# The experts' small side tasks in two parts: what TensorE multiplies for them stands behind the next expert's first up products

## The chip, the core and the metric

The kernel runs on one core of a Trainium2 chip. A core has a matrix engine (TensorE, PE in the profile; its weight loads are shown as PEld), VectorE (DVE), ScalarE (ACT), GpSimd (POOL), and SyncE (SP), which here only issues DMAs. Each engine works through its own list of instructions in order and waits at semaphores for the others. Matrix products land in PSUM, a small memory of banks; everything else lives in SBUF or in device memory (HBM, "dram" in names). The metric is the device time of one execution in microseconds (us). A profiled execution also gives every instruction's start and length, and the TensorE clock that was granted, as a share of full speed.

## The reference

Two layers, on x of 4 x 512 x 512 (2048 tokens of 512):

```python
x = x + _L0_xattn_ref(ctx_1024, _layernorm(x), ...)       # a state-space scan over time
x = x + _L0_ffn_ref(_layernorm(x), gate, gate_up, down, similarity)   # experts
x = x + _L1_xattn_ref(_layernorm(x), ctx_1024, Wq, Wk, Wv, Wo, gq, gk) # attention
x = x + _L1_ffn_ref(_layernorm(x), w1, w2)                 # ternary weights, 8-bit activations
```

The part around the change is the second line. Each token picks 8 of 64 experts by a softmax over gate logits; some of the picks are mapped to a similar expert; then each expert computes on its tokens

```python
gu = lax.ragged_dot(xs, swapaxes(gate_up_proj, 1, 2), group_sizes)   # 512 -> 2 x 192
gate, up = jnp.split(gu, 2, axis=-1)
y = lax.ragged_dot(jax.nn.silu(gate) * up, swapaxes(down_proj, 1, 2), group_sizes)
out = jnp.zeros_like(x).at[tok].add(y * w[:, None])
```

Three things that later stages need are computed beside the experts: the weight of each pick and the row where its y lies; the mean of |w1| and of |w2| and the rounded ternary weights of the last line; and the inverse norms of the attention's keys.

## The kernel before, in words

The order of instructions on each engine is the order in which the Python code calls them: the phase stands under a manual schedule (moe_phase), and no planner moves anything in it. Pools decide only when a buffer may be written again.

The experts' loop (Experts.run_in, lines 1373 to 1391) has 66 turns, one more for each stage of a pipeline over 64 experts. The experts are sorted by size and have fixed room, from 352 rows down to 232, in tiles of 128 rows. Turn i does, in this order:

- issues on POOL's queue the gathers of expert i+2's rows (xg) and weights (wg, wd), four buffers each (line 1223);
- for m = 0, 1, 2: the up products of expert i-1 (gate_up, line 1282, eight instructions into a PSUM tile pg of which there are three), and then the transposes of one tile of expert i's rows (turn_x, line 1266) into a PSUM tile pt, copied to xT by ScalarE, or by VectorE for tile 1 (line 1269). Silu is on ScalarE (1286, 1288), the product h on VectorE (1289, 1291);
- in the first turns, a key task (pk, line 1182);
- the down products of expert i-2 (po, lines 1306 to 1316), whose copies yo are stored to y_dram by SP (1328);
- side tasks from a list (line 1388), until the number done has reached (i-1)/54 of them;
- keys.squares, the sums of squares of the key task's result (kpss, line 1202).

So an expert's h is used one turn after it was made, and so is xT. The PSUM tag "pt" has two buffers in turn; the transposes of the rows, the key tasks and all side tasks share them.

The side tasks are called one after the other, and each ran as a whole. Most have no TensorE work. Those that have some prepare an operand on another engine first:

- many (1470): one small product. Not touched by the change.
- row (1475), twice: VectorE makes a diagonal s_diag, TensorE multiplies ones with it (prow, 1479), VectorE copies the row.
- remap (1497), four times: TensorE transposes four blocks of wt (pwT, 1501), ScalarE copies them to s_wT (1503), TensorE multiplies by the map of experts (pw, 1506), ScalarE copies back to wt (1507).
- mean (1757), twice: VectorE sums the parts of a weight matrix (wone, 1759), TensorE sums over partitions (pm, 1761), VectorE makes the scale of it (1762, 1763). The tasks add and round_ around it read the weights w1 and w2 in eight pieces each.
- key_norms (1551): step 0 loads the sums of squares to krk (SP, 1556); step 1 takes 1/sqrt of them (rsqrt, line 90: a root on ScalarE, for which it loads a table, and five VectorE operations, lines 96 to 100); steps 2 and 3 transpose 128 and 64 columns of it (kpt, 1563), copy them to krows on ScalarE (1565) and store them to r_dram on SP (1570). The pool that holds krows and s_wT has one buffer of each.

After the loop the program reads one number (the blocks of rows that found no room) and branches on it; here the branch is not taken. Attention then starts by gathering y rows (line 1823).

Of the kernel before, what the change touches and what calls it, by code (L numbers as in the profile page):

```python
# [17 lines left out]
F32 = mybir.dt.float32  # L18
# [6 lines left out]
ALU = mybir.AluOpType  # L25
# [4 lines left out]
P = 128  # L30
B, S, DM = 4, 512, 512
NT = B * S // P
NC = DM // P
CTX = 256
EPS = 1e-5
DS, DC, DR = 16, 4, 16
NG = 4
E, TOPK, SEL, FI = 64, 8, 4, 192
# [22 lines left out]
DH = 2048  # L61
# [28 lines left out]
def rsqrt(nc, pool, out, v, tag):  # L90

    shape = list(out.shape)
    r = pool.tile(shape, F32, name=f"rs_r_{tag}", tag=f"rs_r_{tag}")
    t = pool.tile(shape, F32, name=f"rs_t_{tag}", tag=f"rs_t_{tag}")
    nc.scalar.activation(t, v, AF.Sqrt)
    nc.vector.reciprocal(r, t)
    nc.vector.tensor_tensor(t, r, r, ALU.mult)
    nc.vector.tensor_tensor(t, t, v, ALU.mult)
    nc.vector.tensor_scalar(t, t, -0.5, 1.5, ALU.mult, ALU.add)
    nc.vector.tensor_tensor(out, r, t, ALU.mult)  # L100
# [1230 lines left out]
class Experts:  # L1331
# [24 lines left out]
    def run_in(self, ctx, tern, more, late, keys, kv):  # L1356
        cm, ex, st = self.cm, self.ex, self.st
        tc = cm.tc
        ex.sp = ctx.enter_context(tc.tile_pool(name="e_s", bufs=2))
        ex.yp = ctx.enter_context(tc.tile_pool(name="e_y", bufs=3))  # L1360
        ex.ps = ctx.enter_context(tc.tile_pool(name="e_ps", bufs=2, space=PSUM))
        ex.pg = ctx.enter_context(tc.tile_pool(name="e_pg", bufs=3, space=PSUM))
        ex.po = ctx.enter_context(tc.tile_pool(name="e_po", bufs=3, space=PSUM))
        tp = ctx.enter_context(tc.tile_pool(name="e_t", bufs=2))
        kp = ctx.enter_context(tc.tile_pool(name="e_k", bufs=1))
        key_list, ctx_k = key_tasks(keys, self.w, kp, late, ex.ps)
        slots, norms = slot_tasks(cm, self.dr, kv, self.r, more, ex.ps)
        tasks = slots + tern.tasks(tp, ex.ps) + norms
        many = len(tasks)
        done = 0  # L1370
        QUOTA = 54
        self.load_rows(0)
        self.load_rows(1)
        for i in range(E + 2):
            self.load_rows(i + 2)
            self.load_weights(i + 2)
            keys.take()
            for m in range(3):
                if 1 <= i <= E:
                    ex.gate_up(st[i - 1], m)  # L1380
                if i < E:
                    ex.turn_x(st[i], m)
            if i >= 2 and key_list:
                key_list.pop(0)()
            if i >= 2:
                ends = list(range(ROWS[i - 2], ROWS[i - 1], P)) + [ROWS[i - 1]]
                ex.down(st[i - 2], [self.y_dram[r0:r1, :] for r0, r1 in zip(ends, ends[1:])])
                while tasks and done < (i - 1) * many / QUOTA:
                    tasks.pop(0)()
                    done += 1  # L1390
            keys.squares()
        assert not tasks and not key_list
        return ctx_k


# [33 lines left out]
def slot_tasks(cm, dr, kv, r, pool, ps):  # L1429


    nc = cm.nc
    vec, gp, act, pe = nc.vector, nc.gpsimd, nc.scalar, nc.tensor
    c = {}
    codes, chosen = r["codes"], r["chosen"]
    wt = r["weights"] = pool.tile([P, NT, E], F32, name="wt")
# [38 lines left out]
    def row(name):  # L1475
        d = pool.tile([E, E], F32, name="s_diag")
        vec.tensor_scalar(d, cm.ident[0:E, 0:E], c[name], None, ALU.mult)
        pp = ps.tile([P, E], F32, name="prow", tag="pt")
        pe.matmul(pp, cm.ones[0:E, :], d, start=True, stop=True)
        c[name] = pool.tile([P, E], F32, name=f"s_{name}_row")  # L1480
        vec.tensor_copy(c[name], pp)

    def load():
        nc.sync.dma_start(wt, dr["z"][:, :, 0, 0:E].rearrange("t p e -> p t e"))
# [12 lines left out]
    def remap(q):  # L1497
        at = slice(q * NC, (q + 1) * NC)
        pt = ps.tile([E, NC, P], F32, name="pwT", tag="pt")
        for j in range(NC):  # L1500
            pe.transpose(pt[:, j, :], wt[:, q * NC + j, :], cm.ident)
        wT = pool.tile([E, NC, P], F32, name="s_wT")
        act.copy(wT, pt)
        pw = ps.tile([P, NC, E], F32, name="pw", tag="pt")
        for j in range(NC):
            pe.matmul(pw[:, j, :], wT[:, j, :], r["map"], start=True, stop=True)
        act.copy(wt[:, at, :], pw)

    def inside(n):

# [38 lines left out]
    n = sum(c1 - c0 for c0, c1 in cols)  # L1549

    def key_norms(step):
        if step == 0:
            c["rk"] = pool.tile([P, n], F32, name="krk")
            at = 0
            for c0, c1 in cols:
                nc.sync.dma_start(c["rk"][:, at:at + c1 - c0], kv["ms"][:, c0:c1])
                at += c1 - c0
        elif step == 1:
            rsqrt(nc, pool, c["rk"], c["rk"], "k")
        else:  # L1560
            a0, a1 = (step - 2) * P, min((step - 1) * P, n)
            pt = ps.tile([P, P], F32, name="kpt", tag="pt")
            pe.transpose(pt[0:a1 - a0, :], c["rk"][:, a0:a1], cm.ident)
            rows = pool.tile([P, P], F32, name="krows")
            act.copy(rows[0:a1 - a0, :], pt[0:a1 - a0, :])
            at = 0
            for c0, c1 in cols:
                lo, hi = max(at, a0), min(at + c1 - c0, a1)
                if lo < hi:
                    nc.sync.dma_start(kv["r"][c0 + lo - at:c0 + hi - at, :],  # L1570
                                      rows[lo - a0:hi - a0, :])
                at += c1 - c0

    calls = [(load,), (rooms,), (many,), (row, "limit"), (row, "first"), (weigh, 0), (weigh, 1)]
    calls += [(inside, n) for n in range(4)] + [(tops, q) for q in range(NT // NC)]
    calls += [(remap, q) for q in range(NT // NC)]
    calls += [(weight, k, i) for k in range(TOPK) for i in range(3)] + [(finish,)]
    norms = [(key_norms, i) for i in range(2 + -(-n // P))]
    return [[lambda f=f, a=a: f(*a) for f, *a in part] for part in (calls, norms)]

# [136 lines left out]
class Ternary:  # L1717
# [8 lines left out]
    def tasks(self, pool, ps):  # L1726


        cm, nc = self.cm, self.cm.nc

        L = NC * DH // (2 * NC)

        def load(n, c):
            t = pool.tile([P, L], F32, name="wf")
            if n == 0:
                nc.sync.dma_start(t, self.w["w1T"][c // 2 * P:(c // 2 + 1) * P,
                                                   c % 2 * L:(c % 2 + 1) * L])
            else:
                k = L // DM
                src = self.w["w2T"].rearrange("(k p) o -> p k o", p=P)  # L1740
                nc.sync.dma_start(t.rearrange("p (k o) -> p k o", k=k),
                                  src[:, c * k:(c + 1) * k, :])
            return t

        loads = [(n, c) for n in range(2) for _ in range(2) for c in range(2 * NC)]
        ready = []

        def fetch():
            if loads:
                ready.append(load(*loads.pop(0)))  # L1750

        def add(n, c):
            nc.vector.tensor_reduce(self.part[n][:, c:c + 1], ready.pop(0), AX.X, ALU.add,
                                    apply_absolute_value=True)
            fetch()

        def mean(n):
            one = pool.tile([P, 1], F32, name="wone")
            nc.vector.tensor_reduce(one, self.part[n], AX.X, ALU.add)
            pm = ps.tile([P, 1], F32, name="pm", tag="pt")  # L1760
            nc.tensor.matmul(pm, cm.ones, one, start=True, stop=True)
            nc.vector.tensor_scalar(self.mean[n], pm, 1.0 / (DM * DH), EPS, ALU.mult, ALU.max)
            nc.vector.reciprocal(self.ws[n], self.mean[n])

        def round_(n, c):
            t = ready.pop(0)

            nc.vector.tensor_scalar(t, t, self.ws[n], 1.0, ALU.mult, ALU.min)
            nc.vector.tensor_scalar(t, t, -1.0, MAGIC, ALU.max, ALU.add)
            nc.scalar.activation(self.out[n][:, c * L:(c + 1) * L], t, AF.Copy, bias=-MAGIC)  # L1770
            fetch()

        nc.vector.tensor_copy(self.identb, cm.ident)
        calls = [(fetch,), (fetch,)]
        for n in range(2):
            calls += [(add, n, c) for c in range(2 * NC)] + [(mean, n)]
            calls += [(round_, n, c) for c in range(2 * NC)]
        return [lambda f=f, a=a: f(*a) for f, *a in calls]
# [593 lines left out]
```

## Time and profile before

| | |
|---|---|
| three runs | 2628.28, 2637.88, 2644.03 us; median 2637.88 us |
| the profiled execution | 2642.93 us, of which the instructions span 2641.2 us |
| granted TensorE clock, mean over the span | 0.97 |
| scan and routing | 0 to about 640 us |
| experts | about 640 to 1355 us |
| attention and the last layer | about 1360 to 2641 us |
| DMA | 395.77 MB, mean 150 GB/s |

Stretches of the experts' stage (columns: length, busy time of PE, DVE, ACT and POOL, granted clock, share of the time that the DMA engines were busy):

| us | length | PE | DVE | ACT | POOL | clock | DMA |
|---|---|---|---|---|---|---|---|
| 640 to 1262 | 622 | 606.93 | 230.12 | 175.91 | 253.67 | 0.99 | 0.75 |
| 1262 to 1345 | 83 | 77.70 | 21.17 | 23.77 | 27.89 | 0.96 | 0.67 |

An engine's busy time says how much it did, not whether it was waited for. The list of waits puts the idle time of an engine in front of an instruction down to what ended it: "PE pw L1506 <- ACT s_wT L1503" reads: TensorE, at the product pw of line 1506, waited for ScalarE's instruction that writes s_wT in line 1503. A list in order of time gives start and length of runs of equal instructions; their lengths overlap a little with the next run's start, since products are pipelined.

### The profile page before, as it was taken

The numbers are of one execution on the slowest core, as the hardware profiler recorded it, in microseconds if no ns is written. First come the engines' busy times: TensorE is split into PE (matmuls) and PEld (weight loads), VectorE is DVE, ScalarE is ACT, GpSimd is POOL, SyncE is SP. The second block draws the span as 40 slices with busy tenths as digits, with TensorE's granted clock in tenths as the row PEclk, the third lists the DMA queues.
The fourth block names the chain that finished last, engine by engine and source line by source line (L and its number), as shares of the span: only waits on it lengthen the run. The fifth ranks groups of instructions, "written<-read, shape, count | busy, mean of one in ns | idle before, by whom it ended". The sixth has DMA issues, their size and how long they took to land. (4 is left out here: it accounts for less than half of the span.)

```text
span 2641.2 us, 29732 instructions
## 1 busy us (share of the span) xinstructions
PE 2474.5 (94%) x10020; PEld 1404.2 (53%) x10071; DVE 1485.0 (56%) x2562; ACT 1237.6 (47%) x2359; POOL 1180.7 (45%) x1108
## 2 busy tenths in 40 slices
PE   6989899987999999999987999999999999999997
PEld 3555556645555666566653454445555555555543
DVE  6999999854322433344225545456665666555446
ACT  6777777654232222233222444454554555554543
POOL 7999999803333444444325232134322343221112
PEclk8999999988999999999998999999999999999999
DMA  5263444326565677899764534233332443221200
GB/s 206 90 215 113 174 167 161 111 106 201 173 225 171 223 221 259 272 333 328 235 212 139 156 122 122 80 99 98 126 92 84 132 125 95 84 82 59 58 26 21
DMA packets 196143, 395.77 MB, mean 150 GB/s; under 512 B 30339, under 2 KB 71363, under 8 KB 191888
## 3 DMA queue, kind: packets, MB, share of 16 engines
q1 hardware_dynamic: 152926, 238.85, 27.0%
q0 software_dynamic: 41008, 154.76, 18.5%
q8 instruction: 83, 1.36, 0.2%
q10 hardware_dynamic: 2050, 0.18, 0.1%
q14 instruction: 76, 0.62, 0.1%
HBM read 313.88 MB, written 79.82 MB: 149 GB/s over the span
## 5 line engine op out<-in xcount | busy, mean ns | idle before, releaser
L1936 DVE TENSOR_REDUCE mx<-psc 128x1 f32<-128x512 f32 x256 | 176.7, 690 | 460.7 <-PE psc L1933 460.7
L1282 PE MATMUL pg<-xT,wg 128*128 128x284 f32 (+12 forms) x1536 | 399.7, 405 | 2.2 <-ACT xT L1269 1.1
L1282 PEld LDWEIGHTS pg<-xT,wg 128*128 128x128 f32 x1536 | 283.0, 194 | 86.1 <-issue 36.9
L1939 ACT ACTIVATE e<-psc,mx 128x512 f32<-128x512 f32 x256 | 176.0, 687 | 309.2 <-DVE mx L1936 308.9
L492 POOL TENSOR_TENSOR dBu<-bb,du 128x1024 f32<-128x1024 f32 x128 | 303.1, 2388 | 4.4 <-DVE dA L517 3.5
L1223 POOL DMA_INDIRECT xg<-xn_dram,tok x168 | 173.5, 1033 | 215.9 <-PE pt L1266 173.8
L1933 PE MATMUL psc<-kT,qT 128*128 128x512 f32 x512 | 267.5, 604 | 1.0 <-ACT qT L1927 1.0
L1960 PE MATMUL po<-eT,v 128*128 128x512 f32 x512 | 231.4, 595 | 8.5 <-ACT eT L1954 8.4
L1899 PE MATMUL pq<-Wq,xnT 128*128 128x512 f32 x512 | 235.0, 603 | 0.7 <-ACT xnT L1858 0.7
L1969 PE MATMUL px<-Wo,oT 128*128 128x512 f32 x512 | 231.9, 597 | 0.0
L1910 POOL TENSOR_SCALAR qms<-qms 128x4 f32<-128x4 f32 x64 | 24.8, 388 | 413.3 <-DVE qms L1908 412.5
L1953 PEld LDWEIGHTS pet<-ident,e 128*128 128x128 f32 x1024 | 127.9, 142 | 146.3 <-issue 119.9
L503 ACT ACTIVATE dA<-delta,negA 128x512 f32<-128x512 f32 x256 | 176.4, 694 | 52.1 <-DVE hc L518 31.1
L517 DVE TENSOR_TENSOR_SCAN dA<-dA,dBu 128x1024 f32<-128x1024 f32 x80 | 186.5, 2331 | 16.9 <-ACT dA L503 6.6
L1327 DVE COPY yo<-po 128x512 f32<-128x512 f32 x68 | 47.0, 691 | 219.2 <-PE po L1316 219.2
L1960 PEld LDWEIGHTS po<-eT,v 128*128 128x128 f32 x512 | 96.5, 190 | 134.4 <-issue 116.0
L1823 POOL DMA_INDIRECT yg<-y_dram,pos x124 | 125.0, 1008 | 87.3 <-issue 63.4
L1953 PE MATMUL pet<-ident,e 128*128 128x128 f32 x1024 | 155.3, 275 | 7.7 <-DVE e L1945 7.7
L523 PEld LDWEIGHTS yT<-ident,hc 128*128 128x128 f32 x1024 | 117.7, 142 | 79.2 <-issue 40.9
L1223 POOL DMA_INDIRECT wd<-down,widx x64 | 62.7, 980 | 200.5 <-PE po L1316 178.4
L523 PE MATMUL yT<-ident,hc 128*128 128x128 f32 x1024 | 131.6, 276 | 21.5 <-DVE yg L557 9.6
L1954 ACT COPY eT<-pet 128x512 f32<-128x512 f32 x256 | 148.0, 578 | 6.3 <-PE pet L1953 6.1
(355 smaller groups left out, 4375.5 us busy)
## 6 DMA issues: line engine op xcount, KB each, us to landing
y_dram<-yo SPq DMA_DIRECT2D x110, 256.0 KB
bb<-bc_dram SPq DMA_DIRECT2D x16, 1024.0 KB
cb<-bc_dram SPq DMA_DIRECT2D x16, 1024.0 KB
v_dram<-v SPq DMA_DIRECT2D x64, 256.0 KB
k_dram<-k_kT SPq DMA_DIRECT2D x64, 256.0 KB
Wq<-Wq SPq DMA_DIRECT2D x16, 1024.0 KB
kT<-k_dram SPq DMA_DIRECT2D x64, 256.0 KB
rk<-r_dram SPq DMA_DIRECT2D x64, 256.0 KB
```

The lines of the kernel that those rows point to most:

```text
L492: nc.gpsimd.tensor_tensor(dBus[q], st[b]["bb"][i // 2][:, j:j + 2, :], st[b]["du"][c].unsqueeze(1).to_broadcast([P, 2, S]), ALU.mult)
L503: nc.scalar.activation(dAs[q][:, j, :], st[b]["delta"][c], AF.Exp, scale=negA[:, c, n:n + 1])
L517: nc.vector.tensor_tensor_scan(*flat, 0.0, ALU.mult, ALU.add)
L523: nc.tensor.matmul(yT[:, lc, :], t[:, lc * P:(lc + 1) * P], cm.ident, is_transpose=True, start=first and lc == 0, stop=last, skip_group_ch ...
L1223: nc.gpsimd.indirect_dma_start(out=t[0:n, :], out_offset=None, in_=table, in_offset=bass.IndirectOffsetOnAxis(ap=index, axis=0))
L1282: nc.tensor.matmul(pg[:, 0:n], s["wg"][:, c, m * P:(m + 1) * P], s["xT"][:, c, 0:n], start=c == 0, stop=c == NC - 1)
L1899: nc.tensor.matmul(pq.rearrange("p h d -> p (h d)"), xnTs[b * NC + i][:, c, :], s["Wq"][:, c, :], start=c == 0, stop=c == NC - 1)
L1933: nc.tensor.matmul(pscore, st[b, g]["qT"][:, h, i * P:(i + 1) * P], ks[n], start=True, stop=True)
L1936: nc.vector.tensor_reduce(mx, pscore, AX.X, ALU.max, negate=True)
L1953: nc.tensor.transpose(pt[:, kc, :], e[:, kc * P:(kc + 1) * P], cm.ident)
L1960: nc.tensor.matmul(po, v[:, kc, :], eT[:, kc, :], start=kc == 0, stop=kc == KB - 1)
L1969: nc.tensor.matmul(px, oTs[j * HG + h][:, i * P:(i + 1) * P], st[b, g]["Wo"][:, h, :], start=h == 0, stop=h == HG - 1)
```

## The change

A task may now return a function, left, with what remains to be done. The loop keeps it (held), takes no further task in this turn, and calls it in the next turn between the first up products (m = 0) and the first transposes of rows. Row, remap and mean return what begins with their TensorE product; for remap, the transposes and the first copy stay in the task. Step 1 of key_norms returns an empty function, which does nothing but end the turn's tasks. The list of tasks and the pace of 54 are the same; a turn that was cut short is made up for in later ones.

In the lists of the engines this moves: prow (twice), pw (four times) and pm (twice) on TensorE behind the next expert's first up products (the eight instructions of m = 0), with the copies that follow them on VectorE and ScalarE; the four remaps, two of which stood behind one expert, to four experts in a row; the first two products of the task weight on VectorE one expert later; the first kpt with its copy and its store one expert later, so that both kpt stand behind the same expert. POOL's list has the same order as before; on SP only the first store to r_dram changes its place, past two stores to y_dram.

```diff
@@ run_in
+        held = []
@@
             for m in range(3):
                 if 1 <= i <= E:
                     ex.gate_up(st[i - 1], m)
+                if m == 0 and held:
+                    held.pop()()
                 if i < E:
                     ex.turn_x(st[i], m)
@@
-                while tasks and done < (i - 1) * many / QUOTA:
-                    tasks.pop(0)()
+                while tasks and not held and done < (i - 1) * many / QUOTA:
+                    left = tasks.pop(0)()
                     done += 1
+                    if left is not None:
+                        held.append(left)
@@ row
-        pp = ps.tile([P, E], F32, name="prow", tag="pt")
-        pe.matmul(pp, cm.ones[0:E, :], d, start=True, stop=True)
-        c[name] = pool.tile([P, E], F32, name=f"s_{name}_row")
-        vec.tensor_copy(c[name], pp)
+
+        def left():
+            pp = ps.tile([P, E], F32, name="prow", tag="pt")
+            pe.matmul(pp, cm.ones[0:E, :], d, start=True, stop=True)
+            c[name] = pool.tile([P, E], F32, name=f"s_{name}_row")
+            vec.tensor_copy(c[name], pp)
+        return left
@@ remap
-        pw = ps.tile([P, NC, E], F32, name="pw", tag="pt")
-        for j in range(NC):
-            pe.matmul(pw[:, j, :], wT[:, j, :], r["map"], start=True, stop=True)
-        act.copy(wt[:, at, :], pw)
+
+        def left():
+            pw = ps.tile([P, NC, E], F32, name="pw", tag="pt")
+            for j in range(NC):
+                pe.matmul(pw[:, j, :], wT[:, j, :], r["map"], start=True, stop=True)
+            act.copy(wt[:, at, :], pw)
+        return left
@@ key_norms
         elif step == 1:
             rsqrt(nc, pool, c["rk"], c["rk"], "k")
+            return lambda: None
@@ mean
-            pm = ps.tile([P, 1], F32, name="pm", tag="pt")
-            nc.tensor.matmul(pm, cm.ones, one, start=True, stop=True)
-            nc.vector.tensor_scalar(self.mean[n], pm, 1.0 / (DM * DH), EPS, ALU.mult, ALU.max)
-            nc.vector.reciprocal(self.ws[n], self.mean[n])
+
+            def left():
+                pm = ps.tile([P, 1], F32, name="pm", tag="pt")
+                nc.tensor.matmul(pm, cm.ones, one, start=True, stop=True)
+                nc.vector.tensor_scalar(self.mean[n], pm, 1.0 / (DM * DH), EPS, ALU.mult, ALU.max)
+                nc.vector.reciprocal(self.ws[n], self.mean[n])
+            return left
```

More of the change, by code (lines that the diff above doesn't have):

```diff
@@ L1387, in run_in @@
                 ex.down(st[i - 2], [self.y_dram[r0:r1, :] for r0, r1 in zip(ends, ends[1:])])
-                while tasks and done < (i - 1) * many / QUOTA:
-                    tasks.pop(0)()
+                while tasks and not held and done < (i - 1) * many / QUOTA:
+                    left = tasks.pop(0)()
                     done += 1
+                    if left is not None:
+                        held.append(left)
             keys.squares()
-        assert not tasks and not key_list
+        assert not tasks and not key_list and not held
         return ctx_k
```

## The prediction

> **What bounds the kernel now.** I read the page's head and its table of slices first, then TensorE's list of waits in the experts' stage, then the stage's instructions in order of time. The page:
>
> ```profile
> span 2641.2 us, 29732 instructions
> PE 2474.5 (94%) x10020; PEld 1404.2 (53%) x10071; DVE 1485.0 (56%) x2562; ACT 1237.6 (47%) x2359; POOL 1180.7 (45%) x1108
> ```
>
> TensorE is busy 94% of the span, the next engine 56%. The chain of waits cannot be followed through the experts: after them the program branches on a loaded number, and the chain's pieces begin at 1362.08 us. So the stage (about 640 to 1355 us) is judged by who waits for whom in it. From the list of waits between 580 and 1300 us, all engines (microseconds in total, times, longest):
>
> ```profile
> POOL xg L1223 <- PE pt L1266: 173.8, 76, 10.8
> POOL wd L1223 <- PE po L1316: 163.4, 54, 6.5
> ```
>
> The gathers of rows and weights wait for TensorE to give buffers back. In the other direction, TensorE alone:
>
> ```profile
> PE kpt L1563 <- DVE krk L100: 5.3, 1, 5.3
> PE pm L1761 <- DVE wone L1759: 5.2, 2, 3.0
> PE pt L1266 <- DMA xg<-xn_dram,tok: 4.6, 3, 3.0
> PE pw L1506 <- ACT s_wT L1503: 3.9, 4, 1.4
> PE pk L1182 <- DVE xT L1269: 2.9, 1, 2.9
> PE prow L1479 <- DVE s_diag L1477: 2.0, 2, 1.0
> ```
>
> The 4.6 us for a transfer lies before 700 us; later TensorE waits for no DMA. Between 640 and 1262 us it is busy 606.93 of 622 us. It therefore sets the pace, and four of these six rows (kpt, pm, pw, prow) are the small tasks that the change splits. The same places in order of time (start, length, engine and line, work, in brackets the idle time before it):
>
> ```profile
> 674.77 0.40 PE L1479 MATMUL prow<-s_diag,ones 64*128 64x64 f32 x2 [0.97 <-DVE s_diag L1477]
> 675.10 1.05 PE L1202 MATMUL kpss<-ones,k_sq 128*128 128x1 f32 x8
> 676.01 4.14 PE L1282 MATMUL pg<-xT,wg 128*128 128x328 f32 x8
> 680.43 2.37 PE L1282 MATMUL pg<-xT,wg 128*128 128x328 f32 x8
> ...
> 795.07 1.33 PE L1506 MATMUL pw<-map,s_wT 64*128 64x64 f32 x8 [1.37 <-ACT s_wT L1503]
> 796.34 3.69 PE L1282 MATMUL pg<-xT,wg 128*128 128x300 f32 x8
> 800.30 2.19 PE L1282 MATMUL pg<-xT,wg 128*128 128x300 f32 x8
> ...
> 813.29 1.97 PE L1506 MATMUL pw<-map,s_wT 64*128 64x64 f32 x8 [0.72 <-ACT s_wT L1503]
> 815.18 4.26 PE L1282 MATMUL pg<-xT,wg 128*128 128x292 f32 x8
> ...
> 831.39 2.23 PE L1282 MATMUL pg<-xT,wg 128*128 128x292 f32 x8
> ```
>
> Beside the bracketed gap there is a second loss: the same eight products take 3.69 us behind one gap and 2.19 us four microseconds later. The granted clock was 0.83 in 800 to 820 us and 1.00 in 840 to 860. The largest place:
>
> ```profile
> 1268.33 0.45 PE L1563 MATMUL kpt<-ident,krk 128*128 128x128 f32 x1 [5.30 <-DVE krk L100]
> 1268.57 3.41 PE L1282 MATMUL pg<-xT,wg 128*128 128x240 f32 x8
> ...
> 1279.79 1.79 PE L1282 MATMUL pg<-xT,wg 128*128 128x240 f32 x8
> ```
>
> **The change part by part.** The sum is made against the profiled execution's 2642.93 us (2641.2 us span, 1.7 us around it), which is 5.05 us above the median 2637.88 us of the three runs.
>
> *Split tasks.* The preparation on VectorE or ScalarE stays where it was; TensorE passes to the next expert's first up products (pg, about 1.8 to 2.3 us) and does the task's products after them. A gap shorter than that goes whole, a longer one shrinks by one pg. No product is added.
> - row, twice: gaps of 0.97 and 1.03 us, both shorter than pg (2.2 us): 2.00 us.
> - remap, four times: 1.37 + 0.94 + 0.72 + 0.90 = 3.93 us, pg is 2.1 us: all gone. Two stood behind one expert; now each has its own.
> - mean, twice: gaps of 3.00 and 2.19 us. VectorE finishes wone (1090.39 and 1199.60 us) some 2.9 and 2.0 us after the last down product, behind a 1.22 us sum of its own, whatever TensorE does. One pg covers 1.86 and 1.76 us (start to start); 1.14 and 0.43 us stay in front of pm, with the turns queued behind it. Gain 3.62 us.
> - key_norms' rsqrt, which only sends its transpose one expert on: ScalarE loads a table (1263.72, 1.28 us) and takes the root, VectorE needs five operations until 1268.23. TensorE idled 5.30 us and now has an expert's whole work (some 8.7 us) meanwhile. Gain 5.30 us.
>
> Idle time: 14.85 us. The part within mean is the least sure: between 1160 and 1260 us the DMA share is 0.86 to 1.01, and VectorE waits 7.2 us there for ternary weights, so of the second mean's 1.76 us anything from all to nothing may come back as a later wait.
>
> *The clock.* Slow products behind the gaps, by printed lengths against the same shape at full rate: 676.01 us: 4.14 - 2.37 = 1.77. Remap: pw 1.33 - 1.10 and 1.97 - 1.10, pg 3.69 - 2.19 and 4.26 - 2.23, one turn 0.83 - 0.60, together 4.86. At 1268.57 us: 3.41 - 1.79, then a turn 1.06 - 0.60 and a pg 2.30 - 1.79, together 2.59. Sum 9.22 us. Not every gap cost it: the gaps at 693, 830, 1090 and 1199 us, one of them 3.00 us, were followed by full rate. Hence bounds 0 and 9.22. I take 9.22, since no gap is left at these three places, and the low-work stretch that stays (kpss, 1.05 us) stands in front of full-rate pg at 653.67 us too.
> [...]
>
> *Moved and new waits.* Both transposes of key_norms now stand behind one expert. Their copies go to one krows buffer (bufs=1), so ScalarE's second copy waits for the DMA that stores the first, and that DMA is issued on SP behind two y_dram stores, one place later than before. Queued behind the copy on ScalarE: the next silu and xT. TensorE's second turn needs the PSUM buffer that the copy frees. Before, the store to r_dram was issued at 1281.38, 1.73 us after the last down product (1279.65), and that turn began at 3.82 us; with another transpose, 4.07. The landing isn't in the trace: from below, the y_dram store of the chain at 1362.19 us, 2.76 us; from above, the gathers' median of 5.8 us (wd). With some 0.35 us for the copy the turn could start at 4.85 to 7.9 us: a stall of 0.8 to 3.8 us. I take 2.0, nearer to the store, which is the same kind of DMA. A clock loss behind it is 0 (gaps of 2.19 and 3.00 us) to 1.26 us (pk at 665.51 us, behind a gap of 2.92 us, took 3.25 us; 1.99 at 685.76); I take 0.
> - VectorE's first two slot products (1.23 us each) move one expert on and stand there with the reduction (1.22): 3.7 us between the yo copies and h, where two took 2.45 us. VectorE was idle 1.11 us ahead of h, which is used an expert later, so 0; without that cover 1.2 us once.
> - ScalarE's copy of pw now stands behind the silu: 0.37 us ahead of xT, used an expert later: 0.
> - POOL's order is unchanged; its gathers follow TensorE. On SP only that r_dram store moves, past two y_dram stores.
>
> Sum: -14.85 - 9.22 + 2.0 = -22.1 us, so 2620.8 us profiled and 2637.88 - 22.1 = **2615.8 us** as a median.
>
> **Rivals.**
> 1. *The slow products were not the gaps' doing* (small products, or a fixed rhythm of the clock): only the 5.30 us gap frees its 2.59 us. The full-rate rows after 693 and 830 us speak for it, the coincidence at three places against. -14.85 - 2.59 + 2.0 = -15.4 us: 2622.4 us. With no clock back at all and the new stall at 3.8 + 1.26 us: -9.8, 2628.1 us. [...]
> 2. *Hidden anyway*: transfers set the stage's pace and TensorE's gaps merely move. Then about 2637.9 us. For it: DMA share 1.00 at 1160 to 1200 us. Against it: POOL's 337 us of waits for TensorE, and no wait of TensorE for a DMA after 700 us.
> 3. *Slower*: attention's start. Between 1345 and 1440 us TensorE is busy 74.73 of 95 us at a granted 0.86, in short bursts between gathers; a shifted arrival could make the slow clock coincide with all of them. At clock c the busy time is 74.73 x 0.86 / c. To cancel 22 us it must be 95 + 22, so c = 0.55; at 0.50, the lowest granted of any stretch (1268 to 1271 us), it is 128.5 us, net +11 us: 2649 us. Slower than before only below 0.55 throughout, which nothing here shows.
>
> **How the numbers follow.** My forecast 0.70 (its own range 2609 to 2625: at best 14.85 + 9.22 - 0.8 = 23.3 us, at worst 22.1 less 1.76 for the second mean, 1.8 for the longer stall and 1.26 for its clock, 17.3 us; and 5 us either way, since three runs of one kernel spread 16 us). Rival 1: 0.15, half of it beyond 0.5%. Rival 2: 0.10. Rival 3: 0.05. Half a per cent, 13.2 us, is about what runs of this kernel can tell from no change; so the bounds are 2624.7 and 2651.1 us. Faster: 0.70 x 0.97 + 0.075 + 0.02 = 0.77; slower: 0.04; same: the rest, 0.19. The range runs from 2605 to 2630 us: forecast, rival 1 and the noise.
>
> **What would show it.** Right: no idle time in front of prow and pw; about 1.1 and 0.4 us left before pm; kpt twice in a row without a wait; first pg rows at 1.8 to 2.4 us everywhere; the last down product some 22 us earlier, and attention as long as before. The new wait: a turn waiting 1 to 4 us for ScalarE's krows right after the transposes. Wrong: pg rows of 3 to 4 us still behind prow or pw (rival 1), new waits of TensorE for xg, wg or h (rival 2), or a longer stretch between experts and attention (rival 3).

## The result, and the profile after

The changed kernel takes 2615.97 us (median of 8 runs, 2611.18 to 2621.17). The kernel before, run beside it, takes 2642.12 us (median of 8, 2628.28 to 2646.78). The ratio is 0.9907, 95% interval 0.9889 to 0.9924: 24.6 us faster, between 20 and 29 us. The profiled execution spans 2612.2 us.

The head of the page, after:

```profile
span 2612.2 us, 29785 instructions
PE 2469.2 (95%) x10071; PEld 1396.4 (53%) x10071; DVE 1486.6 (57%) x2562; ACT 1237.5 (47%) x2359; POOL 1179.6 (45%) x1108
```

The work is the same; the span is shorter. Three rows of TensorE's list of waits after, between 580 and 1300 us:

```profile
PE pk L1182 <- DVE xT L1269: 2.9, 1, 2.9
PE pt L1266 <- ACT krows L1577: 2.9, 1, 2.9
PE pm L1776 <- DVE wone L1772: 1.3, 2, 1.0
```

The rows of kpt (5.3 us), pw (3.9) and prow (2.0) are gone, pm's went from 5.2 to 1.3 us, and one row is new: a turn of the rows that waits for ScalarE's copy krows. (The row of 4.6 us for transfers, xg, isn't in this execution either; in before it lay ahead of 630 us, in a part that the change doesn't touch.) In order of time, TensorE after, at the first row, at two remaps and at the norms:

```profile
672.51 2.45 PE L1282 MATMUL pg<-xT,wg 128*128 128x328 f32 x8
674.89 0.43 PE L1486 MATMUL prow<-s_diag,ones 64*128 64x64 f32 x2
...
787.92 2.19 PE L1282 MATMUL pg<-xT,wg 128*128 128x300 f32 x8
790.03 1.10 PE L1516 MATMUL pw<-map,s_wT 64*128 64x64 f32 x8
...
801.07 2.13 PE L1282 MATMUL pg<-xT,wg 128*128 128x292 f32 x8
803.13 1.10 PE L1516 MATMUL pw<-map,s_wT 64*128 64x64 f32 x8
...
1252.92 0.44 PE L1575 MATMUL kpt<-ident,krk 128*128 128x128 f32 x2
1253.20 1.79 PE L1282 MATMUL pg<-xT,wg 128*128 128x240 f32 x8
...
1259.91 0.61 PE L1266 MATMUL pt<-ident,xg 112*128 112x112 f32 x4 [2.87 <-ACT krows L1577]
```

There are no brackets in front of prow and pw, and every pg runs at full rate (2.45, 2.19, 2.13 and 1.79 us, where before had 4.14, 3.69, 4.26 and 3.41). What the new wait is made of is seen on ScalarE after:

```profile
1253.55 0.27 ACT L1577 COPY krows<-kpt 128x128 f32<-128x128 f32 x1
1259.60 0.26 ACT L1577 COPY krows<-kpt 64x128 f32<-64x128 f32 x1 [5.78 <-DMA r_dram<-krows]
```

The second copy waited 5.78 us for the store of the first, which SP issued at 1254.64 us: 5.0 us from issue to the second copy's start.

To see where the 29.0 us between the two profiled spans lie, the span is cut at two points: the end of the first shown expert's down products (653.74 us before) and the end of the last one's (1358.80 us before), 62 experts apart.

| us | before | after | difference |
|---|---|---|---|
| ahead of the experts | 653.74 | 651.61 | -2.1 |
| 62 experts | 705.06 | 683.69 | -21.4 |
| behind them | 1282.40 | 1276.90 | -5.5 |

The change touches only the middle row. Whether the other two belong to it is one of the questions below.

### The profile page after: what moved, and what is told of

It reads as the page before. It is cut to its first block, busy times and chain, and to the rows that moved or that the text cites. A ratio compares the mean times of both kernels' runs of the same rounds, so it can differ in the third digit from the quotient of the medians.

```text
span 2612.2 us, 29785 instructions
## 1 busy us (share of the span) xinstructions
PE 2469.2 (95%) x10071; PEld 1396.4 (53%) x10071; DVE 1486.6 (57%) x2562; ACT 1237.5 (47%) x2359; POOL 1179.6 (45%) x1108
## 4 chain that ended last, share of the span: by engine, by line
PE 42%; DVE 3%; DMA 2%; ACT 1%; issue 1%; POOL 1%; DVEq 0%; POOLq 0%; ACTq 0%; SPq 0%
PE po L1976 9%; PE psc L1949 8%; PE px L1985 8%; PE pq L1915 7%; PE pet L1969 4%; PE pf L2085 2%; PE ph L2051 2%; DMA yg<-y_dram,pos 1%; PE pqt L1942 1%; DVE mx L1952 1%; DVE e L1961 1%; PE pk L1182 1%; PE pth L2015 0%; DMA out<-y 0%; DVE x_all L1847 0%
## 5 line engine op out<-in xcount | busy, mean ns | idle before, releaser
L1282 PE MATMUL pg<-xT,wg 128*128 128x284 f32 (+12 forms) x1536 | 392.6, 399 | 1.7 <-ACT xT L1269 1.1
```

The source lines that it names most:

```text
L1282: nc.tensor.matmul(pg[:, 0:n], s["wg"][:, c, m * P:(m + 1) * P], s["xT"][:, c, 0:n], start=c == 0, stop=c == NC - 1)
```

## The experiments

The theory: TensorE's idle time in front of the small products goes, and with it the slow products behind it, which the idle time had caused; a new wait for the single krows buffer costs 2.9 us. Rivals: the slow products had another cause; or the new wait stands for something else that is late. The expectations speak of a stage that begins one expert later and ends at the start of the last down products (692.2 and 670.8 us); its differences are the same as those of the 62 experts, except where the first of them changes.

**The norms' part alone**, on the kernel before:

```diff
+                if m == 0 and held:
+                    held.pop()()
...
             rsqrt(nc, pool, c["rk"], c["rk"], "k")
+            return lambda: None
```

> Only the norms' part of the change on the kernel before: after the inverse root of the keys' norms the turn's tasks end, so both transposes stand behind the next expert; row, remap and mean are whole as before. Measured within the experts' stage, from the key product at 665.5 us (before) to the last down product, which is 692.2 us before and 670.8 us after the whole change. Theory (idle time and the slow clock behind it both go, the new wait for the single krows buffer comes): 5.30 + 2.59 gained, 2.87 lost as in the changed kernel's trace, so the stage is 5.0 us shorter, and TensorE waits 2 to 3.5 us for ScalarE's krows. Rival (the slow products had another cause): 5.30 - 2.87 = 2.4 us shorter, and slow pg products still somewhere near. Second rival (the wait for krows is of the whole change, not of this part): 7.9 us shorter, no wait for krows.

Measured: 62 experts in 701.16 us, 3.9 less than before; ratio 0.998 (0.9961 to 1.0). At the place itself, the two experts concerned are 4.9 us shorter: 8.02 us of idle and slow time went, 3.13 us came. The wait for krows is there, 2.77 us long:

```profile
1275.61 0.60 PE L1266 MATMUL pt<-ident,xg 112*128 112x112 f32 x4 [2.77 <-ACT krows L1571]
```

So the wait belongs to this part, and the theory's 5.0 us hold at the place. The missing 1 us was lost elsewhere, at gaps that this kernel shares with before: here they cost more at row and mean, less at the remaps.

**The remaps alone**, on the kernel before (the loop as above, and remap's product returned as left):

> Only the remap's part on the kernel before: the transposes and the first copy in one turn, the product by the map behind the next expert's first up products, one remap per expert. The rest is whole as before. Same stage (692.2 us before). Theory (idle time and the slow clock behind it): 3.93 + 4.86 = 8.8 us shorter, pg behind pw at 2.1 to 2.2 us each. Rival (slow products had another cause, such as the small products themselves, which are all still there): 3.9 us shorter, with pg of 3 to 4 us near 790 to 830 us.

Measured: 695.79 us, 9.3 less than before; ratio 0.9961 (0.9946 to 0.9976). The four experts at the remaps give 9.1 us of that, no wait for s_wT is left, and the products run at full rate on both sides:

```profile
789.08 2.19 PE L1282 MATMUL pg<-xT,wg 128*128 128x300 f32 x8
791.20 1.10 PE L1513 MATMUL pw<-map,s_wT 64*128 64x64 f32 x8
792.72 2.19 PE L1282 MATMUL pg<-xT,wg 128*128 128x300 f32 x8
```

All small products are still there, so by themselves they don't slow the products beside them.

**The gaps filled.** The kernel before, with useless products in the idle time of row, remap and norms. At the remap, and likewise for the others:

```diff
         pw = ps.tile([P, NC, E], F32, name="pw", tag="pt")
+        for _ in range(2):
+            pe.matmul(pw.rearrange("p c e -> p (c e)"), cm.ident,
+                      r["codes"].rearrange("p t e -> p (t e)")[:, 0:NC * E], start=True, stop=True)
```

> The kernel before, undivided, but TensorE multiplies something nobody reads while it waits: two products of 256 columns in front of each row and each remap product, five of 512 columns in front of the norms' first transpose, written to the PSUM tile that the real product then overwrites. The gaps stay as long as they were and are filled with work; mean's are left as they are. Same stage (692.2 us before). If the slow products behind the gaps come from TensorE's idle time, they go: 1.77 + 4.86 + 2.59 = 9.2 us, less about 0.5 us where the filling is longer than a gap: 8 to 9.5 us shorter, first pg at 1.8 to 2.4 us everywhere. If they come from the small products, from a fixed rhythm or from anything else than idle time: no shorter than 0 to 1 us, pg of 3 to 4 us stay.

Measured: 695.04 us, 10.0 less than before, with more work done; ratio 0.9951 (0.993 to 0.9972). That is a little above the 8 to 9.5 expected; of the 10.0 us, 9.2 lie at the places of the change. The filled gaps, TensorE:

```profile
807.97 1.13 PE L1510 MATMUL pw<-codes,ident 128*128 128x256 f32 x4
809.03 1.10 PE L1513 MATMUL pw<-map,s_wT 64*128 64x64 f32 x8
810.06 2.23 PE L1282 MATMUL pg<-xT,wg 128*128 128x292 f32 x8
...
1254.81 4.56 PE L1571 MATMUL kpt<-codes,ident 128*128 128x512 f32 x10
1260.13 0.33 PE L1574 MATMUL kpt<-ident,krk 128*128 128x128 f32 x1 [0.76 <-DVE krk L100]
1260.30 1.79 PE L1282 MATMUL pg<-xT,wg 128*128 128x240 f32 x8
```

The operand arrives as late as before, but the pg behind it takes 2.23 us where it took 4.26, and 1.79 where it took 3.41. The three pg behind the remaps take 2.29, 2.23 and 2.23 us; before had 3.69, 4.26 and 2.23, and a granted clock of 0.83 in 800 to 820 us. Behind none of the seven filled gaps is a pg slow; in each of the three executions of before (below) it is behind at least four of the seven. This settles the cause: the slow products came from TensorE's idle time. How a gap of 0.72 to 1.37 us slows the products behind it, no trace here shows.

**The remaps whole again, one per expert**, in the changed kernel:

```diff
-        def left():
-            pw = ps.tile([P, NC, E], F32, name="pw", tag="pt")
-            for j in range(NC):
-                pe.matmul(pw[:, j, :], wT[:, j, :], r["map"], start=True, stop=True)
-            act.copy(wt[:, at, :], pw)
-        return left
+        pw = ps.tile([P, NC, E], F32, name="pw", tag="pt")
+        for j in range(NC):
+            pe.matmul(pw[:, j, :], wT[:, j, :], r["map"], start=True, stop=True)
+        act.copy(wt[:, at, :], pw)
+        return lambda: None
```

> The changed kernel with the remaps whole again, each in one turn and still one per expert: four gaps of 0.7 to 1.4 us come back, apart from each other; all else stays changed. Same stage (670.8 us in the changed kernel). Idle time alone: 3.9 us longer. If each short gap also brings the slow clock: 4 x about 2 us more, 12 us longer. If only gaps close together or long enough do (two remaps stood behind one expert before): 3.9 to 6 us longer. The kernel before lost 4.86 us of clock at three places of this kind and nothing at the fourth.

Measured: 692.94 us, 9.3 more than the changed kernel; ratio to before 0.9929 (0.9902 to 0.9955). 7.6 us of it lie at the remaps, 1.9 us at the wait for krows: 0.2 us because it is longer, 1.7 us of slow products behind it, which the first execution of the changed kernel did not have. That lies between the answers expected. TensorE at three of the four:

```profile
792.68 1.10 PE L1514 MATMUL pw<-map,s_wT 64*128 64x64 f32 x8 [0.94 <-ACT s_wT L1511]
793.71 3.98 PE L1282 MATMUL pg<-xT,wg 128*128 128x300 f32 x8
...
808.57 1.10 PE L1514 MATMUL pw<-map,s_wT 64*128 64x64 f32 x8 [0.94 <-ACT s_wT L1511]
809.60 2.23 PE L1282 MATMUL pg<-xT,wg 128*128 128x292 f32 x8
...
836.64 1.10 PE L1514 MATMUL pw<-map,s_wT 64*128 64x64 f32 x8 [0.94 <-ACT s_wT L1511]
837.67 3.65 PE L1282 MATMUL pg<-xT,wg 128*128 128x292 f32 x8
```

The gaps are equal, 0.94 us, in equal surroundings; behind two of the four pg is slow, behind the other two (the third, not shown, has 2.23 us) it isn't. So a gap of 0.94 us may be followed by slow products and need not.

**Both kernels again, with traces.**

> The kernel before once more, with a trace. For what lies outside the experts' stage: between the two profiled executions shown, the part up to the key product at 665.5 us differs by 2.1 us and the part behind the last down product by 5.5 us (1283.5 and 1278.0 us) though the change touches neither. If that is chance, another execution of the same kernel differs from its first by as much, 2 to 6 us in each part. If the change does something there, this one repeats 665.5 and 1283.5 within 1 us.

> The changed kernel once more, with a trace. As for the kernel before: if the 2.1 and 5.5 us outside of the experts' stage are chance, this execution differs by 1 to 6 us in those parts; the stage itself should repeat 670.8 us within 1 us, and the wait for krows of 2.9 us should come again, varying with the landing of a DMA by 1 us or so.

> The kernel before a third time, with a trace, for the size of the slow products behind the same gaps: the first execution had 9.3 us of them in the places that the change touches, the second 17.2 us, with the idle time equal. If the slow clock falls behind a gap by chance, this execution lies anywhere between about 5 and 20 us, with other places hit than in the first two, and idle time of 14.8 us again.

Measured, beside the first executions:

| us | before, 1st | 2nd | 3rd | after, 1st | 2nd |
|---|---|---|---|---|---|
| ahead of the experts | 653.74 | 653.99 | 650.03 | 651.61 | 644.95 |
| 62 experts | 705.06 | 712.42 | 705.98 | 683.69 | 682.98 |
| behind them | 1282.40 | 1278.79 | 1279.39 | 1276.90 | 1278.27 |

Both outer rows move within one kernel, the first by up to 6.7 us, the last by up to 3.6; over all twelve profiled executions of this study, whose kernels are alike in these parts, the first lies between 644.95 and 655.28 us, the last between 1276.90 and 1284.50. The -2.1 and -5.5 us are within that. The middle row of before moves as well, by 7.4 us, and here the places tell why. For each place (two experts at row, four at the remaps, two at mean, two at the norms), how much longer its experts are than in the changed kernel's first execution:

| us longer | row | remap | mean | norms | sum |
|---|---|---|---|---|---|
| before, 1st | 3.5 | 9.1 | 3.6 | 4.8 | 20.9 |
| before, 2nd | 6.8 | 8.9 | 8.3 | 4.8 | 28.8 |
| before, 3rd | 6.8 | 5.6 | 6.9 | 4.8 | 24.2 |
| gaps filled | 1.8 | 4.2 | 3.6 | 2.2 | 11.7 |

The idle time in them is the same in all three, about 12 us more than in the changed kernel (2.0 for row, 3.5 to 3.9 for remap, 5.2 - 1.3 for mean, 5.3 - 2.9 for norms: 11.8 to 12.2). The rest I count as slow products: 8.7, 17.0 and 12.4 us. For the first execution the printed lengths give 9.22 us, as the prediction has it, so the two counts agree within 0.5 us. The first execution had none behind the gaps of mean; the second had them. TensorE at the first mean, second execution of before:

```profile
1093.98 0.56 PE L1761 MATMUL pm<-wone,ones 128*128 128x1 f32 x2 [3.00 <-DVE wone L1759]
1094.40 3.87 PE L1282 MATMUL pg<-xT,wg 128*128 128x264 f32 x8
```

The same pg took 2.03 us in the first execution, behind a gap of the same 3.00 us; with what follows, this expert took 3.1 us longer in the second. The mean of the three sums is 24.6 us.

**Two buffers for krows**, in the changed kernel:

```diff
-            rows = pool.tile([P, P], F32, name="krows")
+            if step == 2:
+                rows = pool.tile([P, P], F32, name="krows")
+            else:
+                rows = pool.tile([E, NC, P], F32, name="s_wT")[:, 0, :]
```

> The changed kernel, with the second krows copy in another buffer (that of s_wT, long free by then), so that ScalarE does not wait for the store of the first. Same stage (670.8 us in the changed kernel). Theory: the 2.87 us in which TensorE waits for ScalarE's krows go, nothing comes in their place, the stage is 2.9 us shorter, 667.9 us. Rival (something else is late there, such as xT or silu after the table load one expert earlier, or the DMA of weights): a new wait of 1 us or more near it, under 1.5 us gained. Against the kernel before some 27 us in all.

Measured: 680.57 us, 3.1 less than the changed kernel's 683.69; the wait for krows is gone and none came in its place. Ratio to before 0.9899 (0.9881 to 0.9917), 2613.48 us.

**Mean's product behind the second up products**, on top of that:

```diff
-                if m == 0 and held:
-                    held.pop()()
+                if held and m == held[0][0]:
+                    held.pop()[1]()
...
-            return left
+            return 1, left
```

> As the kernel with two krows buffers, and mean's product stands one step later, behind the next expert's second up products (m = 1) and not the first. Theory: the 1.02 and 0.32 us left in front of pm go too, the stage is 1.3 us shorter still, 666.5 us. Rival (VectorE or the ternary tasks behind pm get late, since the scale of the weights comes 2.3 us later): no gain, TensorE or VectorE waits near the first rounding tasks.

Measured: 678.59 us, 2.0 less; 1.26 and 0.56 us less at the two places. Ratio to before 0.9892 (0.9874 to 0.9911), 2612.76 us. TensorE's waits of this kernel from 640 us to attention's first key product, all that the list names:

```profile
PE pk L1182 <- DVE half L1828: 4.5, 1, 4.5
PE pk L1182 <- DVE xT L1269: 2.9, 1, 2.9
PE pg L1282 <- ACT h L1293: 0.4, 1, 0.4
```

The first is the beginning of attention. Both steps are seen in the traces; in the runs' times they lie within the intervals of the changed kernel.

**The task rooms cut in two as well:**

```diff
         vec.tensor_scalar(nov, nov, MAGIC, MAGIC, ALU.add, ALU.subtract)
+        return lambda: None
+
+    def firsts():
+        place, room = r["place"], r["room"]
+        t = pool.tile([E, 1], F32, name="s_t")
         first = c["first"] = pool.tile([E, 1], F32, name="s_first")
...
-    calls = [(load,), (rooms,), (many,), (row, "limit"), (row, "first"), (weigh, 0), (weigh, 1)]
+    calls = [(load,), (rooms,), (firsts,), (many,), (row, "limit"), (row, "first"), (weigh, 0), (weigh, 1)]
```

> As the kernel with two krows buffers and the later mean, and the task rooms, some fifty tiny VectorE operations in a row, is cut into two tasks behind two experts. It is the last place of the experts' stage with a wait of TensorE over 1 us: 2.9 us for VectorE's xT in front of a key product, in every kernel so far, and 1.7 us of slow products behind it. Theory: both go, the stage is 4.6 us shorter than with the later mean (666.8 us to the end of its last down product, from where that key product started there, so to be read from the expert's down products ahead of it). Rival: half of the operations are still too many, a wait of about 1 us stays at one or both experts; 1 to 3 us shorter. In time, about 2608 us, if before is about 2640.

Measured: 677.55 us, only 1.0 less than with the later mean; 2614.23 us, ratio to before 0.9886 (0.9864 to 0.9909). The wait of 2.9 us and the slow products behind it went, 4.8 us at the place. But another place gave 3.9 us back, with a wait where neither theory nor rival had put one. TensorE, in the part with ternary weights:

```profile
1215.95 3.20 PE L1282 MATMUL pg<-xT,wg 128*128 128x248 f32 x8 [2.62 <-ACT h L1293]
```

and VectorE a little ahead of it:

```profile
1208.54 0.79 DVE L1792 TENSOR_SCALAR wf<-wf,ws 128x1024 f32<-128x1024 f32 x1 [3.32 <-issue]
...
1211.01 0.75 DVE L1792 TENSOR_SCALAR wf<-wf,ws 128x1024 f32<-128x1024 f32 x1 [0.95 <-DMA wf<-w2T]
```

One rounding of weights began 3.3 us late, the next waited 0.95 us for its DMA, ScalarE's copies came after them, and silu and h stood behind those. The DMA engines are busy 98% of the time from 1110 to 1210 us, as in the changed kernel. The order of the tasks explains part of it. The cut moved the later tasks against the experts: two roundings now stand behind each of two experts in a row (VectorE at 1196.29, 1197.79, 1208.54 and 1211.01 us), where the kernel with the later mean has two, one and two. A rounding's weights are loaded only when the rounding two before it is done, so SP issued the second pair's loads from 1198.87 us on, 9.7 us ahead of the first of that pair; with the later mean such a load, issued at 1192.43 us, held its rounding until 1201.23 us, 8.8 us. That the first rounding of the pair waited for its load is likely but not named by the trace, and with one execution the size of the wait stays open. The last three versions lie between 2612.76 and 2614.23 us by median, and the runs don't tell them apart.

## Why the prediction was right

*The bound.* TensorE sets the pace of the stage: right. Whatever idle time went there came out of the experts' stretch in full: 15.1 us of idle time went (16.4 to 1.3) and 2.9 us of new wait came; the four places are 20.9 us shorter, which leaves 8.7 us for the slow products, and their printed lengths in before give 9.2. The whole stretch is 21.4 us shorter, against 22.1 predicted from the first of these two traces. Rival 2, transfers, did not show in the changed kernel; its mechanism is near, as the last experiment has it.

*Row and remap.* 2.00 and 3.93 us, covered whole: right, no idle time in front of prow and pw.

*Mean.* Left in front of pm: 1.02 and 0.32 us, predicted 1.14 and 0.43. Right.

*Norms.* The gap of 5.30 us goes: right.

*The clock.* The cause, idle time, was right, and the filled gaps show it; rival 1 is out. The size, 9.22 us, was that of one execution. I took the gaps without slow products (693, 830, 1090, 1199 us) as places that never cost any; the second and third executions have slow products behind three of these four. In three executions they come to 8.7, 17.0 and 12.4 us, so the term was too small by some 3 to 4 us against the middle one.
Rival 1's time rests on the gap of 5.30 us alone costing slow products, 2.59 us; no run shows a gap's length deciding it. They stood behind two of four gaps of 0.94 us, and behind a gap of 3.00 us in one execution and not in another.

*The new wait.* Its place, cause and bounds (0.8 to 3.8 us) were right; 2.0 was too low. It took 2.87, 2.77, 3.1 and 2.7 us in the four traces that have it, since the second copy could start only some 5 us after the store's issue (5.0 in the first of them) and not 2.76: I had taken the value nearer to a store that ran after the experts. Whether the gathers beside it or the two larger stores ahead of it on the queue made the difference, no run shows. Slow products behind the wait, costed at 0, came in two of the four and cost 1.7 us in each, more than the bound of 1.26.

*The number.* The predicted time agrees better than the working deserves. The median of before is 4.2 us higher with eight runs than with three, and the gain is 24.6 us by the ratio and 26.2 by the medians, not 22.1; the two cancel, and that is luck. The 29.0 us between the first two profiled executions are more than the change's: 7.6 us of them lie where it does nothing.

## What to carry to other kernels

Where one engine sets the pace and works through its list in order, a small task with a hand-over in the middle costs the hand-over each time (here 0.72 to 5.30 us); splitting it so that the engine's next regular work stands between its halves takes that cost out (here 15.1 of 16.4 us), and the gain can be read off the list of waits. For TensorE the gap was not the whole price here: add the slow products behind it (8.7 to 17.0 us), and take them from several executions, since a gap of 3.00 us was followed by none in one and by 3.1 us of them in the next. After a split, look at which tasks now stand behind the same piece of work and share a buffer of one: here that alone gave back 2.9 us.

## What was not expected

- Idle gaps of TensorE of 0.94 us were followed by pg products of 3.65 and 3.98 us in place of 2.2, in two of four like places. A gap of 3.00 us was followed by full rate in one execution and by 3.87 us in place of 2.03 in another.
- The part ahead of the experts, alike in all kernels here, differs by 10 us over the twelve executions, the part behind them by 8 us, more than most parts of this change are worth. Stretches cut at landmarks and compared place by place resolved 1 us where the runs' times, with intervals of some 4 to 7 us either way, did not.
- A 64 KB store behind two of 256 and 240 KB on the same queue took 5.0 us from its issue until the engine that waited for it went on.
